# Joint statistics for the first four token tiles, and transposes of the identity on TensorE at the start of a transformer block

## The chip, the cores and the metric

The kernel runs on one core of a Trainium2 chip. The metric is the device time of one launch in microseconds (us). A core has five engines that run their own instruction queues: TensorE (PE; its weight loads are shown as PEld), VectorE (DVE), ScalarE (ACT), GpSimd (POOL) and SyncE (SP), which here issues the DMA transfers. Engines wait for each other by semaphores.

## The reference

The reference is one transformer block on 2048 tokens of width 512, in float32. Cut to what matters here:

```python
xn = _layernorm(x, axis=-1)
x = x + _L0_attn_ref(xn, w_qkv, w_o) + _L0_ffn_ref(xn, gate, up, down)   # 4-bit FFN weights

def _layernorm(x, axis=-1, eps=1e-05):
    m = jnp.mean(x, axis=axis, keepdims=True)
    v = jnp.var(x, axis=axis, keepdims=True)
    return (x - m) / jnp.sqrt(v + eps)
```

Attention is causal with 16 heads of width 32; the feed-forward part has width 4096. Both take the same normalized tokens.

## The kernel before, in words

The tokens stand in 16 tiles of 128 tokens by 512 values, and four tiles make a token block (`b` = 0 to 3). All instructions are recorded in a fixed order by hand, so each engine runs its own in the order in which the Python code calls them.

At the start, constants are made: GpSimd writes `ident`, the 128 by 128 identity (line 130). SyncE issues the loads: token tiles `x0` to `x3`, the projection weights `wqk` of the first group of heads, the value weights `wv` in four parts, then `x4` to `x15` (lines 62 to 71). The tiles use eight buffers in turn, so the load of `x8` waits until `x0` has been normalized, and so on.

A token block then goes through three helpers:

- `statistics(b, first, n)` computes mean and variance of `n` tiles on VectorE (`st`, line 468, and `mv`, line 469, for each tile), and then the inverse standard deviation for all `n` at once: `ve` (line 471), a square root on ScalarE (`sd`, line 473), and five small operations on VectorE (`q` and `rstd`, lines 476 to 481) that refine and invert it.
- `normalize(b, i)` writes the normalized tile `xn` on VectorE (line 489), in one of two buffers (`turn12`, `turn13`).
- `flip(b, i)` transposes `xn` on TensorE in four pieces of 128 by 128, with `ident` as the other operand, to the PSUM tile `ptx` (line 505), and ScalarE copies that to `xnT` (line 508).

For the first block this is done for two tiles at a time:

```python
for i in range(4):
    if i % 2 == 0:
        statistics(0, i, 2)
    normalize(0, i)
    flip(0, i)
```

Then follows a loop over the four blocks. For each it records the next block's `statistics` and first `normalize`, two projections of the present block (`project`, line 166, queries and keys of the first heads, each with a copy on ScalarE at line 178 or 180), and then four steps of transposes of the next block, scores (line 210), their row maxima on VectorE and values (`ps_v`, line 516). A projection is four float32 matmuls of 128x128 by 128x512, which the profile shows as eight instructions.

After this stage come the attention of the pairs of heads, the output projection and the feed-forward part, in which no line is touched by the change. PSUM tiles named `t` come from a pool of three buffers, `ps_t`, which the attention uses in turn.

Of the kernel before, what the change touches and what calls it, by code (L numbers as in the profile page):

```python
# [46 lines left out]
P = 128  # L47
# [7 lines left out]
NK = H // P  # L55
# [23 lines left out]
def block_kernel(  # L79
# [10 lines left out]
    nc = tc.nc  # L90
# [4 lines left out]
    def turn_tile(i, name, dtype=F32, shape=(P, TB)):  # L95
        return turns.tile(list(shape), dtype, tag=f"turn{i}", name=name)
# [17 lines left out]
    with (  # L114
# [14 lines left out]
        ident = const.tile([P, P], F32, tag="ident", name="ident")  # L129
# [69 lines left out]
        def tile_of(pool, name):  # L199
            return pool.tile([P, TB], F32, tag="s" if pool is ps_s else "t", name=name)  # L200
# [262 lines left out]
        def statistics(b, first=0, n=4):  # L463
            key = f"{b}_{first}"
            mv = small.tile([P, n, 2], F32, tag="mv", name=f"mv{key}")
            for i in range(n):
                st = small.tile([P, 6], F32, tag="st", name=f"st{key}_{i}")
                nc.vector.bn_stats(st, xs[4 * b + first + i])
                nc.vector.bn_aggr(mv[:, i, :], st)
            ve = small.tile([P, n], F32, tag="ve", name=f"ve{key}")  # L470
            nc.vector.tensor_scalar(ve, mv[:, :, 1], EPS, None, ALU.add)
            sd = small.tile([P, n], F32, tag="sd", name=f"sd{key}")
            nc.scalar.activation(sd, ve, AF.Sqrt)

            q = small.tile([P, n], F32, tag="q", name=f"q{key}")
            nc.vector.reciprocal(q, sd)
            nc.vector.tensor_tensor(q, q, ve, ALU.mult)
            nc.vector.tensor_tensor(q, q, sd, ALU.add)
            nc.vector.tensor_scalar(q, q, 0.5, None, ALU.mult)
            rstd = small.tile([P, n], F32, tag="rstd", name=f"rstd{key}")  # L480
            nc.vector.reciprocal(rstd, q)
            for i in range(n):
                mvs[b, first + i], rstds[b, first + i] = mv[:, i, 0:1], rstd[:, i : i + 1]
# [1 line left out]
        xns = {}  # L485

        def normalize(b, i):
            xn = turn_tile(12 + i % 2, f"xn{b}_{i}", shape=(P, NK, 8, 16))
            nc.vector.tensor_scalar(
                xn,  # L490
                xs[4 * b + i].rearrange("p (b r k) -> p k r b", b=16, r=8),
                mvs[b, i],
                rstds[b, i],
                ALU.subtract,
                ALU.mult,
            )
            xns[b, i] = xn

        def flip(b, i):

            bank = i % 2 if b == 0 else b < 3
            pt = ps_m.tile([P, TB], F32, tag=f"m{int(bank)}", name=f"ptx{b}_{i}")
            xn = xns.pop((b, i))
            for k in range(NK):
                nc.tensor.transpose(  # L505
                    pt[:, k * P : (k + 1) * P], xn[:, k].rearrange("p r b -> p (r b)"), ident
                )
            nc.scalar.copy(
                xnT[b][:, :, i * P : (i + 1) * P],
                pt.rearrange("p (k t) -> p k t", k=NK),  # L510
            )

        def value_halves(t):
# [11 lines left out]
            nc.scalar.copy(v[t // 4][:, t % 4, :], ps)  # L525
            yield

        for i in range(4):
            if i % 2 == 0:
                statistics(0, i, 2)  # L530
            normalize(0, i)
            flip(0, i)

        later = [(1, b, which) for b in range(NTB) for which in range(2)]
        for b in range(NTB):
            n = first[b]
            if b + 1 < NTB:
                statistics(b + 1)
                normalize(b + 1, 0)
            project(0, b, 0)  # L540
            project(0, b, 1)
            for i in range(4):
                if b + 1 < NTB:
                    flip(b + 1, i)
                full_width = [value_halves(4 * b + i)] * 2
                if b >= 2:
                    full_width += [project_halves(*later.pop(0))] * 2
                for j in range(b + 1):
                    rows_when_due()
                    tiles = [score_rows(0, n, ps_s), score_rows(1, n, ps_t)]  # L550
                    for p in range(2):
                        maxima(p, n, tiles[p])
                    if j == 0 and i < 3 and b + 1 < NTB:
                        normalize(b + 1, i + 1)
                    n += 1
                    for _ in range(-(-len(full_width) // (b + 1 - j))):
                        next(full_width.pop(0))
# [13 lines left out]
        for m in range((NP - 2) * STEPS):  # L571
            p, n = divmod(m, STEPS)
# [36 lines left out]
            if own in places and og + 2 < NOG:  # L609
                b, which = places[own]  # L610
                project(og + 2, b, which, tile_of(ps_s, f"ps_qk{og + 2}_{b}_{which}"))
            if own in places_own and og > 0 and og + 1 < NOG:
                b, which = places_own[own]
# [56 lines left out]
        for s, n in enumerate(together):  # L670
# [21 lines left out]
            if early and s % 2 == 0 and not diagonal(together[s + 1]):  # L692
                i, k = early.pop(0)
                b = ORDER[i]
# [178 lines left out]
    with tc.manual_schedule():  # L873
# [13 lines left out]
        for n, t in enumerate(order):  # L887
# [13 lines left out]
            if n < 8:  # L901
                b, k = ORDER[2 + n // NK], n % NK
# [180 lines left out]
```

## Time and profile before

| what | value |
|---|---|
| median of 3 runs | 1975.38 us (1973.5 to 1975.81) |
| profiled execution | 1972.27 us, of which the span is 1970.2 us |
| TensorE busy in the span | 1934.5 us (98%) |
| VectorE, ScalarE, GpSimd busy | 67%, 56%, 47% |
| data moved by DMA | 39.86 MB |
| mean granted TensorE clock | 0.999 |

Busy time is the time in which an engine has an instruction at work; matmuls overlap each other, and a busy TensorE is not TensorE at its peak. Times in the timeline and the chain of waits are microseconds from the start of the span: first the start, then the time taken, then engine, tile and line. A line of the timeline may sum up several instructions (`x8`), and in square brackets is the engine's idle time before it and what ended it. In a table of windows, PEclk is the granted clock of TensorE as a share of full speed, the third value from the end of a line.

### The profile page before, as it was taken

The numbers are of one execution on the slowest core, as the hardware profiler recorded it, in microseconds if no ns is written. First come the engines' busy times: TensorE is split into PE (matmuls) and PEld (weight loads), VectorE is DVE, ScalarE is ACT, GpSimd is POOL, SyncE is SP. The second block draws the span as 40 slices with busy tenths as digits, with TensorE's granted clock in tenths as the row PEclk, the third lists the DMA queues.
The fourth block names the chain that finished last, engine by engine and source line by source line (L and its number), as shares of the span: only waits on it lengthen the run. The fifth ranks groups of instructions, "written<-read, shape, count | busy, mean of one in ns | idle before, by whom it ended". The sixth has DMA issues, their size and how long they took to land.

```text
span 1970.2 us, 32411 instructions
## 1 busy us (share of the span) xinstructions
PE 1934.5 (98%) x11648; PEld 1182.9 (60%) x11648; DVE 1326.7 (67%) x2706; ACT 1104.2 (56%) x2299; POOL 927.6 (47%) x1055
## 2 busy tenths in 40 slices
PE   7999999999999999999999999999999999999998
PEld 3433333333333332247888888888888888888886
DVE  5657665656555764187777676777777777777774
ACT  2112665656556666625666666666666666666664
POOL 1001555545445653155655454555555555555451
PEclk9999999999999999999999999999999999999999
DMA  3000000000000000020000000000000000000002
GB/s 128 0 11 11 2 2 1 1 12 2 1 1 12 2 1 21 18 79 22 22 18 23 19 22 20 21 20 20 19 22 20 21 21 21 21 19 24 18 5 86
DMA packets 55392, 39.86 MB, mean 20 GB/s; under 512 B 14784, under 2 KB 47552, under 8 KB 55232
## 3 DMA queue, kind: packets, MB, share of 16 engines
q1 hardware_dynamic: 55232, 37.81, 6.5%
q8 instruction: 91, 1.49, 0.3%
q14 instruction: 69, 0.57, 0.1%
HBM read 33.55 MB, written 4.19 MB: 19 GB/s over the span
## 4 chain that ended last, share of the span: by engine, by line
PE 94%; ACT 3%; POOL 1%; issue 1%; DVE 1%; DMA 0%; DVEq 0%; ACTq 0%; POOLq 0%
PE gu L935 24%; PE gu L948 12%; PE pd L998 12%; PE av L344 10%; PE ps_s L210 8%; PE pd L1010 6%; PE ps_qk L166 6%; PE ps_t L281 4%; PE ps_t L296 3%; PE ps_v L516 3%; PE po L890 3%; ACT prob L310 2%; POOL added L396 1%; PE ptx L505 0%; PE pm L262 0%
## 5 line engine op out<-in xcount | busy, mean ns | idle before, releaser
L935 PE MATMUL gu<-xh,gu 128*128 128x512 f32 x1024 | 403.9, 394 | 0.0
L935 PE MATMUL gu<-lm,gu 128*128 128x512 f32 x1024 | 403.7, 394 | 0.0
L234 DVE TENSOR_REDUCE tops<-ps_s 128x1 f32<-128x512 f32 x384 | 243.7, 682 | 160.4 <-PE ps_s L210 122.3
L1019 DVE SCALAR_TENSOR_TENSOR acc<-pd,acc 128x512 f32<-128x512 f32 x512 | 317.1, 682 | 2.4 <-PE pd L1010 2.4
L980 POOL TENSOR_TENSOR parts<-inter,hi 128x512 fp32r<-128x512 f32 x128 | 171.1, 1336 | 278.2 <-DVE hi L976 271.9
L310 ACT ACTIVATE prob<-ps_t 128x512 f32<-128x512 f32 x384 | 205.7, 596 | 145.6 <-PE ps_t L296 102.1
L210 PE MATMUL ps_s<-qk,qk 32*128 32x512 f32 (+3 forms) x1280 | 286.4, 576 | 0.0
L948 PE MATMUL gu<-lm,gu 128*128 128x512 f32 x1024 | 279.7, 395 | 0.0
L972 DVE SCALAR_TENSOR_TENSOR inter<-gu,gate 128x512 f32<-128x512 f32 x128 | 88.5, 692 | 274.9 <-PE gu L948 274.9
L296 PE MATMUL ps_t<-qk,qk 32*128 32x512 f32 (+3 forms) x1280 | 271.2, 538 | 0.0
L1005 ACT ACTIVATE pd<-pd 128x512 f32<-128x512 f32 x512 | 263.4, 583 | 1.1 <-PE pd L998 1.1
L344 PE MATMUL av<-prob,v 128*32 128x128 f32 (+3 forms) x1856 | 257.6, 425 | 5.5 <-ACT both L430 4.2
L998 PE MATMUL pd<-wd,parts 128*128 128x512 f32 x1024 | 259.6, 396 | 0.0
L942 ACT ACTIVATE gu<-gu 128x512 f32<-128x512 f32 x256 | 148.7, 581 | 188.2 <-PE gu L935 188.1
L396 POOL TENSOR_TENSOR added<-prob,prob 128x512 f32<-128x512 f32 x144 | 179.6, 1268 | 115.9 <-ACT prob L310 115.4
L948 PEld LDWEIGHTS gu<-lm,gu 128*128 128x128 f32 x1024 | 192.0, 188 | 47.1 <-issue 0.2
L935 PEld LDWEIGHTS gu<-lm,gu 128*128 128x128 f32 x1024 | 191.9, 187 | 46.6 <-POOL wd L805 0.2
L998 PEld LDWEIGHTS pd<-wd,parts 128*128 128x128 f32 x1024 | 192.3, 188 | 45.8
L935 PEld LDWEIGHTS gu<-xh,gu 128*128 128x128 f32 x1024 | 192.0, 188 | 45.7 <-ACT wd L804 0.2
L344 PEld LDWEIGHTS av<-prob,v 128*32 128x32 f32 x1856 | 67.2, 108 | 206.2 <-issue 147.5
L229 DVE CUSTOM_DVE_ANT_0 ps_s<-ps_s,mask_qk 128x128 f32<-128x128 f32 (+3 forms) x256 | 120.8, 516 | 92.0 <-PE ps_t L296 52.3
L979 ACT CAST parts<-hi 128x512 fp32r<-128x512 f32 x128 | 79.7, 623 | 173.2 <-DVE hi L976 171.4
(106 smaller groups left out, 2942.8 us busy)
## 6 DMA issues: line engine op xcount, KB each, us to landing
pk<-packed SPq DMA_DIRECT2D x96, 128.0 KB, 2.2
sc<-scales SPq DMA_DIRECT2D x512, 8.0 KB, 1.6
x<-x SPq DMA_DIRECT2D x16, 256.0 KB, 3.5
acc<-x SPq DMA_DIRECT2D x16, 256.0 KB, 3.3
sc<-scales SPq DMA_DIRECT2D x256, 16.0 KB, 1.7
out<-acc SPq DMA_DIRECT2D x16, 256.0 KB, 2.2
wqk<-w_qk SPq DMA_DIRECT2D x4, 512.0 KB, 3.7
wv<-w_v SPq DMA_DIRECT2D x4, 256.0 KB, 5.4
```

What stands on the lines that cost most here:

```text
L210: nc.tensor.matmul(ps[:, :w], lhsT=qT[p // 2, qb][rows, i * P : (i + 1) * P], rhs=kT[p // 2, c][rows, :w], start=True, stop=True,)
L234: nc.vector.tensor_reduce(top, ps[:, :w], AX.X, ALU.max)
L296: nc.tensor.matmul(ps[:, c0:], lhsT=kT[p // 2, kt // 4][rows, (kt % 4) * P : (kt % 4 + 1) * P], rhs=qT[p // 2, qb][rows, c0:], start=False ...
L310: nc.scalar.activation(prob[:, h, :], ps, AF.Exp)
L344: nc.tensor.matmul(avs[p, qb][D * j : D * (j + 1), c0:c1], lhsT=v[kt // 4][:, kt % 4, D * head : D * (head + 1)], rhs=prob[:, h, c0:c1], s ...
L396: nc.gpsimd.tensor_tensor(t, prob_a[:, h], prob_b[:, h], ALU.add)
L935: nc.tensor.matmul(ps, lhsT=parts[:, i, k], rhs=mov, start=(k == 0 and i == 0), stop=(k == NK - 1 and i == 1),)
L948: nc.tensor.matmul(ps, lhsT=gu[g, m, j][:, 2, k], rhs=lm[b, k][1], start=False, stop=(k == NK - 1), skip_group_check=True,)
L980: nc.gpsimd.tensor_tensor(parts[:, 1], inter, high, ALU.subtract)
L998: nc.tensor.matmul(po, lhsT=parts[:, part, i * P : (i + 1) * P], rhs=w[:, part], start=(part == 0), stop=(part == 1),)
L1005: nc.scalar.activation(po, po, AF.Copy, scale=HIGH_SCALE)
L1019: nc.vector.scalar_tensor_tensor(acc[t], po, SUM_SCALE, acc[t], ALU.mult, ALU.add)
```

## The change

The statistics of the first block's four tiles are taken in one call, ahead of the four normalizations. The first block's normalized tiles get four buffers instead of two. And TensorE is given 36 transposes of the identity, written to a PSUM tile `idle` that nobody reads, ahead of the first tokens, three more after each of the first three tiles' transposes, and six after the last. `idle` is a tile of the pool `ps_t`, and so takes one turn of its three buffers.

```diff
         def normalize(b, i):
-            xn = turn_tile(12 + i % 2, f"xn{b}_{i}", shape=(P, NK, 8, 16))
+            xn = turn_tile(12 + i % (2 if b else 4), f"xn{b}_{i}", shape=(P, NK, 8, 16))
...
+        idle = tile_of(ps_t, "idle")
+
+        def stay_busy(n):
+
+            for _ in range(n):
+                nc.tensor.transpose(idle[:, :P], ident, ident)
+
+        stay_busy(36)
+        statistics(0)
         for i in range(4):
-            if i % 2 == 0:
-                statistics(0, i, 2)
             normalize(0, i)
             flip(0, i)
+            stay_busy(3 if i < 3 else 6)
```

In the instruction order of the two kernels, TensorE has 51 transposes more (36, 3, 3, 3 and 6), VectorE has six instructions fewer and ScalarE one fewer. The first transpose of the identity waits for GpSimd alone. The two normalizations that waited for TensorE to release a buffer of `xn` no longer do. All other instructions stand in the same order with the same waits.

## The prediction

> **What bounds the kernel.** I read the page's chain and slices first, then the chain of the first 50 us in order of time, then the timeline of the start.
>
> ```profile
> PE   7999999999999999999999999999999999999998
> ...
> PE 94%; ACT 3%; POOL 1%; issue 1%; DVE 1%; DMA 0%; DVEq 0%; ACTq 0%; POOLq 0%
> ```
>
> TensorE is on the chain for 94% of the span, and only the first slice (49 us) has room. The edit touches nothing behind the first projection, so it is worth what it moves that projection, and how fast that runs. The chain of 0 to 50 us:
>
> ```profile
> 0.80 2.64 DMA x<-x
> 3.47 0.71 DVE st L468
> ...
> 6.64 0.75 DVE xn L489
> 7.39 0.14 issue
> 7.53 1.95 PE ptx L505 x8
> 9.50 0.58 ACT xnT L508
> 10.09 0.11 ACT sd L473
> ...
> 11.30 0.75 DVE xn L489
> 12.05 0.14 issue
> 12.18 1.96 PE ptx L505 x8
> 14.16 0.59 ACT xnT L508
> 14.76 0.04 issue
> 14.80 5.22 PE ps_qk L166 x8
> 20.04 0.61 ACT qk L178
> 20.65 0.04 issue
> 20.69 3.71 PE ps_qk L166 x8
> ```
>
> Until 14.80 us the chain is VectorE's: statistics of two tiles, two normalized tiles, then both again, with the transposes and a ScalarE copy behind each pair. From 14.80 it is TensorE with its copies, and no load is in it after the first token tile. So a shift at 14.80 reaches the end whole: I find nothing behind that would absorb it.
>
> The same eight matmuls take 5.22 us, and 3.71 us right after. The timeline of weight loads shows the step:
>
> ```profile
> 16.67 0.34 PEld L166 LDWEIGHTS ps_qk<-xnT,wqk 128*128 128x128 f32 x1 [0.52 <-issue]
> 17.52 0.34 PEld L166 LDWEIGHTS ps_qk<-xnT,wqk 128*128 128x128 f32 x1 [0.52 <-issue]
> 18.13 0.19 PEld L166 LDWEIGHTS ps_qk<-xnT,wqk 128*128 128x128 f32 x1 [0.27 <-issue]
> 18.56 0.19 PEld L166 LDWEIGHTS ps_qk<-xnT,wqk 128*128 128x128 f32 x1 [0.24 <-issue]
> ```
>
> Starts stand 0.85 us apart, then 0.61, then 0.43: TensorE doubles its pace at about 17.9 us, some 3.07 us after its first dense matmul. The transposes show the same two paces: starts 0.213 us apart in the two early groups, 0.109 us in the groups from 25.07 on. The column of granted clock says 1.00 even for 14.80 to 16.50, so it doesn't show this step at the start; it does show the way back, at the end:
>
> ```profile
> 1963.40:1966.88 3.48, 1.73 (x7) 0.70 (x5) 2.75 (x5) 1.17 (x3) 0.00 (x0) 1.00 0.74 273
> 1966.88:1970.20 3.32, 0.00 (x0) 0.00 (x0) 0.00 (x0) 0.00 (x0) 0.00 (x0) 0.50 0.54 201
> ```
>
> The last matmul starts at 1964.62, and at 1966.88 the granted clock is 0.50.
>
> **VectorE's part.** One set of six small operations and one square root go (in the second pair, 9.69 to 11.30 us), and statistics of x2 and x3 come ahead of the first normalization. Statistics start 0.82, 0.80 and 0.79 us apart, so x3's would start at 5.88; its landing is recorded at 6.07 us (x2's at 4.83, in time), so it starts at 6.10. That added wait holds what is queued behind it on VectorE, all on the path, and costs 0.2 us. From a last statistics to ve is 0.91 us (15.03 to 15.94), from ve to xn 1.44 (first pair) to 1.54 us (four wide, with one more wait in it): xn0 starts at 8.45 to 8.55, I take 8.48, and the next 0.65 us apart, xn3 at 10.4 instead of 11.95. From xn's start to its first transpose is 0.88 us (6.64 to 7.53), so the first real transpose can go at 9.36 us.
>
> Hidden: statistics of the next block start at 11.1, when x4 has landed (10.97) and x5 to x7 come at 11.66 to 13.01 us, before each is read; their xn is wanted by TensorE only after both projections. The loads of x8 and later wait on SyncE for xn0 and on (x8 now until 9.2 us instead of 7.4), and behind them stand the other loads; DMA is full with earlier tiles until about 13 us, and x8 is first read at 42.5 us. Were that cover gone, 2 us would show. ScalarE loses one 0.2 us operation; GpSimd's work is unchanged. Two more xn buffers take away two waits.
>
> **TensorE's part.** The 36 transposes need only the identity, written by 1.37 us; the first starts at about 1.46. Nothing real is queued behind them before 9.36. At the slow pace they last 36 x 0.213 = 7.67 us, until 9.15, 0.2 us before the tokens. That is 2.5 times the 3.07 us after which the matmuls sped up. Whether transposes bring the faster pace can't be read here: two groups stood dense for 1.7 us each without it, which is shorter than 3.07. I bound it both ways.
>
> If they count, the step comes after 3 to 6 us, the 36 end between 6.6 and 8.3 us, and a tile costs TensorE (4 + 3) x 0.109 + 0.03 = 0.79 us, a little over VectorE's 0.65. So the tiles go at 9.36, 10.15, 10.94 and 11.73; the last transpose of ptx3 starts at 12.07, the copy 0.31 later (25.46 to 25.76) at 12.37, the projection 0.64 after that (14.16 to 14.80), at 13.01. The six last idle ones end at 12.8 and are under the copy. The projection starts 1.79 us earlier, and runs 3.74 us to its copy (20.69 to 24.43) instead of 5.24 (14.80 to 20.04): 1.50 us. Sum **-3.29 us**.
>
> If they don't, the pace stays slow, a tile costs 7 x 0.213 + 0.03 = 1.52 us, TensorE and no longer VectorE sets the order, ptx3 starts at 9.36 + 3 x 1.52 = 13.92, and the six last ones hold the projection until 13.92 + 0.88 + 6 x 0.213 = 16.08: **+1.28 us** at least.
>
> [...]
>
> I take the first value: in both states matmuls and transposes change pace together and by the same factor (0.85 to 0.43, 0.213 to 0.109), and 36 stand dense for longer than the matmuls needed.
>
> **Time.** The profiled execution took 1972.27 us, 2.07 outside its span; less 3.29 it is 1968.98. The three runs' median is 1975.38, 3.1 us above that execution, from which I carry the difference over: 1972.1 us. With a pace change that came later, all eight matmuls of the first projection would start 0.853 us apart and take some 7.2 us instead of 5.24; executions like that would gain 1.79 + 3.46 = 5.25 us. [...] About 0.2% (3.95 us) is what a measurement of this kernel can tell from no change.
>
> **Rivals.**
> 1. *Transposes don't count* (chance 0.25). For it: no speed-up in either early group. Price +1.28 us; if the slow stretch also takes in the whole first projection, 1.96 more, +3.2. The slower side: it decides when starts stay above about 0.175 us apart, since 9.36 + 31 x 0.175 = 14.8. 1976.7 to 1978.6 us.
> 2. *The pace is lost again in the gap between the 36 and the tokens* (0.12). The gap is 1.1 to 2.7 us, and at the end of the trace the clock was halved within 2.3 us of the last matmul's start. Then the tokens' transposes start slow and speed up after 3 to 6 us: a speed-up at 12.4 gives a start at 14.5 and a fast projection, -1.8; one that comes only just before the projection -0.2. I take -1.0: 1974.4. Against it: with the step at 4.2 us and later the TensorE stands still for under 3 us.
> 3. *The edit moves nothing* (0.03): the extra transposes start late, or x3 lands later. 1975.4.
>
> **Numbers.** Forecast 1972.1 with 0.60. Its gain is 2.8 to 5.25 us by execution, and it passes 3.95 in somewhat under half: 0.27 of the 0.60. Faster: 0.27 + 0.02 (rival 2) + 0.01 = 0.30. Slower by over 0.2%: 0.05 of rival 1, with the three runs' own scatter (2.3 us), + 0.02. The rest, 0.63, within 0.2%. The forecast's own range is 1969.6 (gain 5.25, less 0.5 of scatter) to 1973; up to 1977.4 takes in rival 2 and over half of rival 1, leaving out some 2 in 10.
>
> **What would show it.** Right: statistics x4 in a row, xn at about 8.5; the 36 end between 6.6 and 8.3; ptx groups of 0.6 us, not 0.85; first projection from 13.0, weight loads 0.43 apart from the first on, and 3.7 us. Wrong: the 36 at 0.213 to the end at 9.15, ptx groups 1.5 us apart, projection after 16; or a fast stretch and slow tokens (rival 2). A time beyond 1979 or below 1969 would mean that something behind 50 us moved, which I can't see.

## The result, and the profile after

| | median | runs |
|---|---|---|
| before | 1975.58 us | 1972.21 to 1976.27, 12 runs |
| changed | 1971.66 us | 1968.85 to 1972.91, 12 runs |

The ratio is 0.9981, with a 95% interval of 0.9973 to 0.9988: some 3.9 us faster (2.4 to 5.3). 3.29 us were forecast, 1972.1 us. The profiled execution of the changed kernel took 1971.69 us, with a span of 1969.6, only 0.6 us shorter than before's; the reason is a fall of the clock at the start of the attention, shown below.

From the profile's page of the changed kernel, the slices of TensorE and the chain's shares:

```profile
PE   8999999999999999999999999999999999999998
...
PE 94%; ACT 3%; POOL 1%; issue 1%; DVE 0%; DMA 0%; SPq 0%; DVEq 0%; ACTq 0%; POOLq 0%
```

The first slice goes from 7 to 8 tenths busy, the transposes of the identity included; the rest is as before. The chain of waits of the first 30 us (start, time, what):

```profile
2.18 4.13 DMA x<-x
6.30 0.02 issue
6.33 0.70 DVE st L468
...
8.74 0.75 DVE xn L489
9.49 0.04 issue
9.53 0.66 PE ptx L505 x4
10.19 0.33 PE idle L533 x3
10.51 0.44 PE ptx L505 x4
...
12.04 0.44 PE ptx L505 x4
12.48 0.66 PE idle L533 x6
13.13 0.02 issue
13.15 3.71 PE ps_qk L166 x8
16.87 0.02 issue
16.89 0.61 ACT qk L178
17.50 0.04 issue
17.54 3.71 PE ps_qk L166 x8
```

The chain now begins with the load of the fourth tile (6.30), goes through one set of statistics, and then through TensorE. The first projection starts at 13.15 instead of 14.80 and takes 3.71 instead of 5.22 us. The next block's first transposes start at 21.92 instead of 25.07: **3.15 us earlier**, and from here on both kernels do the same.

A table of windows of the changed kernel (busy time and count for each engine; the granted clock is third from the end) shows the step of the pace under the 36 transposes, and what comes later:

```profile
1.40:5.30 3.90, 3.88 (x18) 3.88 (x19) 2.15 (x8) 0.68 (x1) 2.28 (x6) 1.00 0.78 252
5.40:7.40 2.00, 2.00 (x19) 1.85 (x17) 1.63 (x5) 0.00 (x0) 0.00 (x0) 1.00 0.99 359
...
189.80:196.40 6.60, 6.28 (x35) 1.82 (x29) 2.76 (x5) 2.30 (x6) 3.63 (x4) 0.50 0.00 0
196.60:200.00 3.40, 3.23 (x40) 1.23 (x34) 1.41 (x4) 2.51 (x7) 1.21 (x2) 1.00 0.00 0
```

Eighteen transposes touch the first 3.9 us, nineteen the next 2.0. In the trace their starts stand 0.213 us apart until 5.3 and 0.109 us from 5.5 on, and the trace's record of the granted clock begins at 5.39 us. That record starts with the first change of the clock, and the table shows 1.00 for all time ahead of it, whatever the pace; in before's trace it starts at 17.87 us, where the matmuls doubled their pace. Up to 5.39 us TensorE had done nothing but transpose the identity. The third line is new: from 189.7 to 196.5 us the granted clock is 0.50, at the start of the attention loop. Before's profile has 1.00 there:

```profile
189.80:196.40 6.60, 4.63 (x37) 1.73 (x36) 4.03 (x8) 4.16 (x9) 2.49 (x2) 1.00 0.15 61
```

### The profile page after: what moved, and what is told of

It reads as the page before. It is cut to its first block, busy times and chain, and to the rows that moved or that the text cites. A ratio compares the mean times of both kernels' runs of the same rounds, so it can differ in the third digit from the quotient of the medians.

```text
span 1969.6 us, 32503 instructions
## 1 busy us (share of the span) xinstructions
PE 1941.5 (99%) x11699; PEld 1188.9 (60%) x11699; DVE 1325.7 (67%) x2700; ACT 1104.7 (56%) x2298; POOL 927.8 (47%) x1055
## 4 chain that ended last, share of the span: by engine, by line
PE 94%; ACT 3%; POOL 1%; issue 1%; DVE 0%; DMA 0%; SPq 0%; DVEq 0%; ACTq 0%; POOLq 0%
PE gu L943 24%; PE gu L956 12%; PE pd L1006 12%; PE av L344 10%; PE ps_s L210 8%; PE pd L1018 6%; PE ps_qk L166 6%; PE ps_t L281 4%; PE ps_t L296 3%; PE ps_v L516 3%; PE po L898 3%; ACT prob L310 2%; POOL added L396 1%; PE ptx L505 0%; PE pm L262 0%
```

## Experiments

**Joint statistics alone** (e1): the joint statistics and the four buffers stay, the transposes of the identity go, and with them the tile `idle` and its turn in the pool.

```diff
-        idle = tile_of(ps_t, "idle")
...
-        stay_busy(36)
         statistics(0)
         for i in range(4):
             normalize(0, i)
             flip(0, i)
-            stay_busy(3 if i < 3 else 6)
```

> The joint statistics and the four buffers of xn alone, no transposes of the identity. Theory (the transposes bring TensorE to its fast pace, the joint statistics only bring xn earlier): xn0 starts at 8.7 us as in the changed kernel, but the transposes of the tokens stand 0.213 us apart, so a tile costs 0.85 us and the last one starts at 9.53 + 0.24 + 14 x 0.213 = 12.75; copy at 13.2, first projection at 13.85 (before 14.80, after 13.15), and its matmuls start slowly, 0.85 us apart for 3 to 6 us, so that it takes 5.2 to 7.2 us to its copy instead of 3.74. The next block's first transposes then come at 24.1 to 26.1 us (before 25.07, after 21.92): some 1 us gained, or as much lost. Rival (joint statistics alone bring the gain, the pace would have come anyway): next block's transposes at about 22 us.

Its timeline of TensorE:

```profile
10.00 3.73 PE L505 MATMUL ptx<-ident,xn 128*128 128x128 f32 x16 [10.00 <-DVE xn L489]
14.41 1.98 PE L166 MATMUL ps_qk<-xnT,wqk 128*128 128x512 f32 x4 [0.68 <-ACT xnT L508]
```

The tokens' sixteen transposes are slow, 0.213 us apart, as expected, and the projection starts at 14.41 (0.47 of its delay is a later first tile, 10.00 instead of 9.53). But it is fast from the first matmul: the pace changed at 14.33 us in the record. Sixteen slow transposes in one piece, 3.3 us, had brought it, just in time. Next block's transposes: 23.17, 1.90 us earlier than before. I had expected at most 1. So joining the statistics does two things: it brings the last tile earlier, and it puts the transposes in one dense piece. Its single run took 1970.26 us.

**The transposes of the identity alone** (e2): statistics in pairs and two buffers, as before.

> The 51 transposes of the identity alone; statistics in two pairs and two buffers of xn as before. Theory with the pace held: xn2 and xn3 as before at 11.3 and 11.95, last transposes of ptx3 at 13.3, copy 13.6, projection at 14.25 and fast (3.74): next block's first transposes at 23.0 us, 2.1 earlier than before and 1.1 later than after. Theory with the pace lost: between the pairs TensorE stands still from about 9 to 12.2 us, and if that is long enough the second pair is slow again (0.213 us apart), the projection starts at 15.4 to 15.8 and its matmuls are slow: next block's first transposes at 25.7 or later. Which of the two it is tells how long a gap the pace outlasts.

```profile
8.81 0.60 PE L505 MATMUL ptx<-ident,xn 128*128 128x128 f32 x4
9.25 0.49 PE L533 MATMUL idle<-ident 128*128 128x128 f32 x3
12.25 0.63 PE L505 MATMUL ptx<-ident,xn 128*128 128x128 f32 x4 [2.51 <-DVE xn L489]
...
13.47 0.82 PE L533 MATMUL idle<-ident 128*128 128x128 f32 x6
14.31 1.98 PE L166 MATMUL ps_qk<-xnT,wqk 128*128 128x512 f32 x4
```

The pace came at 6.86 us and outlasted the gap between the pairs (2.51 us). The projection starts at 14.31 (expected 14.25), next block's transposes at 23.08 (expected 23.0): 1.99 us earlier than before. The two parts alone give 1.90 and 1.99, together 3.15, since both remove the same 1.50 us of slow matmuls. Counted once, that leaves 2.39; the other 0.76 lies in the start of e1's projection, which was late by 0.47 us for its first tile and by 0.79 for its slow transposes, and 0.49 of that is in e2's gain already. Its single run, 1972.85 us, has the fall of the clock at the start of the attention in it (191.2 to 198.0 us), as the changed kernel's profile has, and e1's hasn't; so the times of single runs can't be set against each other, and the place of the next block's transposes can.

**Eight or twenty in front instead of 36** (e3, e5):

```diff
-        stay_busy(36)
+        stay_busy(8)       # e5: stay_busy(20)
```

> The changed kernel with 8 instead of 36 transposes of the identity in front; all else as in it. They end at 1.43 + 0.24 + 7 x 0.213 = 3.2 us, and TensorE then stands still for 6.3 us. Theory (it is the length of dense work that brings the pace): the tokens' transposes and those of the identity between them are slow, a tile costs 7 x 0.213 = 1.5 us, ptx3 starts at about 14.0 unless the pace comes within that stretch, projection between 14.5 and 16.3: this is the slower side of the prediction, next block's first transposes at 23.3 (pace comes before the projection) to 26.6 us. Rival (any early use of TensorE is enough, or the pace depends on the time since the start): as the changed kernel, 21.9 us.

> The changed kernel with 20 instead of 36 transposes of the identity in front. They end at 5.6 us if all are slow, earlier only if the pace comes within them; then TensorE stands still for some 4 us, where it was 2.0 us in the changed kernel and 2.75 us between the two pairs with the identity's transposes alone, and neither lost the pace. Theory (a gap of a whole stretch of 3.4 us or more takes the pace back, or too few transposes don't bring it): the tokens' transposes start 0.213 us apart, and the projection starts at 14.5 or later, next block's first transposes at 23 us or later. Rival (the pace outlasts 4 us): as the changed kernel, 21.9 to 22.3 us.

With eight, the transposes of the first three tiles are slow and TensorE sets the order: groups start at 9.74, 11.29 and 12.78, 1.5 us apart, as the slower rival of the prediction had it. The pace comes at 13.46, just before the projection at 15.16; next block's at 23.93. With twenty it comes at 6.67, after the last one has started (5.53), and is gone again when the tokens come. Windows of the run with twenty:

```profile
6.70:10.05 3.35, 0.06 (x1) 0.07 (x2) 2.75 (x10) 0.20 (x1) 0.00 (x0) 1.00 1.03 388
10.10:13.45 3.35, 3.35 (x17) 3.35 (x18) 3.28 (x7) 1.17 (x2) 0.00 (x0) 0.50 1.05 391
13.55:20.00 6.45, 5.74 (x25) 3.20 (x24) 3.32 (x12) 1.98 (x4) 0.00 (x0) 1.00 0.41 139
```

An empty stretch of 3.41 us at the full clock, then one at half clock under dense slow transposes, then full again; next block's transposes at 24.04. So an early use of TensorE wasn't enough in these two runs: the eight brought no faster pace ahead of the tokens, and what the twenty brought was gone after the gap. Gaps of 2.0 us in the changed kernel and 2.5 us in e2 did no harm, 4.0 us lost the pace in this execution. The single runs took 1973.57 us (e3, with the clock's fall at the attention, 191.0 to 197.8) and 1971.23 us (e5, without it).

**More transposes at the start of the attention** (e4, on the changed kernel; e7, on before). There TensorE waits for exponentials between narrow matmuls (1.19, 0.54 and 0.53 us in before's profile).

```diff
+        idle_av = ps_m.tile([P, TB], F32, tag="m0", name="idle_av")
+        fill = {0: 10, 1: 5, 2: 5}
         for m in range((NP - 2) * STEPS):
...
             rows_when_due()
...
             later_on(3, attend_diagonal, p, n, prob)
...
+            for _ in range(fill.get(m, 0)):
+                nc.tensor.transpose(idle_av[:, :P], ident, ident)
```

> The changed kernel with 10, 5 and 5 transposes of the identity more behind the first three steps of the attention loop, where TensorE waits 1.19, 0.54 and 0.5 us for exponentials. In the profiled execution of the changed kernel the granted clock is 0.50 from 189.7 to 196.5 us, in that of before it isn't; the transposes of the second block stand 3.15 us earlier in the changed kernel, at 196 us only 0.7 us earlier. The changed kernel's runs have two levels, 1969 and 1972 us. Theory (the lower clock there is the difference of the levels, and it comes when a stretch of some 3.4 us has too little TensorE work): the granted clock stays at 1.00 from 185 to 197 us in this kernel, its runs are all at 1969 to 1969.7 us, median 2.5 us under the changed kernel's 1971.66 and 6 us under before. Rival (the levels have another cause, and the drop costs nothing in the end): runs still at 1969 and 1972, or all 1 to 2 us above these for the added work.

> The kernel before with nothing changed but the 10, 5 and 5 transposes of the identity behind the first three steps of the attention loop. Theory (before loses the granted clock there too, in most of its executions, and its two levels of 1975.5 and 1972.2 us are with and without that): the granted clock stays at 1.00 from 185 to 200 us, median 1972.3 us, some 3 us under before, though the start is as before; what is left of spread comes from the slow stretch at the start. Rival (the fill helps the changed kernel only, because its attention starts earlier): median as before, 1975.

From the first matmul of the attention to the next transposes of `parts` (line 262), the same work takes 8.38 us in before (188.05 to 196.43), 10.81 in the changed kernel's profile with the lower clock (184.89 to 195.70), and 8.39 with the fill on either kernel (185.14 to 193.53 and 188.35 to 196.74). So the lower clock there costs 2.4 us and the fill nothing. That too little work in some 3.4 us brings the lower clock was the expectation's theory; what these profiles show is that it didn't come with the fill. e4 ran at 1968.97 to 1969.50 us but for one run at 1971.03, median 1969.37, ratio to before 0.9976 (0.9966 to 0.9986): the level above 1971.6, which 7 of the changed kernel's 12 runs had, is in none of these nine. The mean granted clock on record says the same of every run: 0.998 in those seven, 0.999 or 1.000 in the five others and in all of e4's (6.83 us at half clock take 0.0017 off the mean).

On before the expectation was missed: median 1973.71 beside 1973.91 for before on the same chip, ratio 0.9996 (0.9987 to 1.0005). What the fill took away is the top: 12 of before's 27 runs there are over 1975 us, all with a mean clock of 0.998; none of e7's 11 is over 1974.3, and none has a mean clock below 0.999. So before, too, has executions in which the clock falls, though its profile is none of them. What was wrong is where the others lie: ten of the eleven are at 1973.1 to 1974.3, and one is at 1972.4. The profile shows one reason, another place where the clock falls:

```profile
752.00:755.60 3.60, 2.64 (x32) 0.96 (x28) 2.29 (x7) 3.12 (x7) 0.87 (x3) 1.00 0.00 0
755.70:759.00 3.30, 3.30 (x16) 0.64 (x16) 2.58 (x4) 1.94 (x4) 2.15 (x3) 0.50 0.00 0
```

Against before's profile, which has 1.00 there, it is 0.31 us late ahead of this stretch (749.21 for 748.90) and 1.99 behind it (759.19 for 757.20): 1.7 us lost. Whether that makes up the rest of its spread isn't shown.

**Joint statistics with the fill** (e8): e1 with the same fill, which leaves the start alone to differ.

> The joint statistics and four buffers with the fill in the attention loop, without the transposes of the identity at the start. In its one execution without the fill, 16 slow transposes of the tokens stood dense for 3.3 us and brought the pace just ahead of the projection, which then ran fast: next block's first transposes at 23.2 us. Theory (that hangs on when in those 3.4 us the tokens come, and varies by execution): times from 1969.5 (pace before the projection) to 1971.5 us (after 3 us of slow matmuls), median 1 to 2 us over the changed kernel with the fill (1969.4). Rival (the tokens' own transposes always bring the pace, the identity's are needless): median 1970.3 at most and little spread.

Median 1970.58 us, from 1969.95 to 1974.05; six runs lie at 1969.9 to 1970.6, three at 1972.2 to 1972.3, two over 1973. Here the tokens' own transposes must bring the pace. In the profiled execution they did at 13.06, ahead of the projection; that they come too late in the runs above 1972 is likely, but no profile of such a run shows it. Beside before with the fill on the same chip (1973.71) joint statistics give about 3.1 us by medians. Against the changed kernel with the fill (1969.37, on another chip) the identity's transposes give 1.2 us more; 0.73 of it stands in the two profiles (next block's transposes at 22.94 and 22.21), and the runs above 1972 are gone. On a third chip the changed kernel with the fill had a median of 1970.32 (e11 below), so this 1.2 is no firm number.

**Two versions meant to be faster** (e6, e10), and the changed kernel and e4 again beside the second (e9, e11). e10 has the fill, 44 transposes in front, none between the tiles; e6 also moves two loads to ScalarE's queue.

```diff
-        stay_busy(36)
+        stay_busy(44)
...
-            stay_busy(3 if i < 3 else 6)
+        stay_busy(6)                      # behind the loop
...
-            nc.sync.dma_start(out=xt, ...)
+            queue = nc.scalar if t in (1, 3) else nc.sync      # e6 alone
+            queue.dma_start(out=xt, ...)
```

> A version meant to be faster than both: the changed kernel with the fill, 44 instead of 36 transposes of the identity in front, none between the tiles and six at the end, and the loads of x1 and x3 issued by ScalarE's queue, so that four loads are issued by 1.7 instead of 2.6 us. x3 was waited for until 6.1 to 6.7 us in the runs with joint statistics. Theory: x3 lands by 5.5 us, xn0 starts at 8.1 instead of 8.7, the tiles follow VectorE's 0.65 us instead of 0.76, so ptx3's last transposes start 1 us earlier; next block's first transposes at 20.9 us, median 1968.4 us (1969.4 with the fill alone). Rival (the loads share the same bandwidth and x3 lands no earlier; the thinner stretch between tiles loses the pace): 1969.2 to 1971.

> The changed kernel itself, on one chip with the two versions below, for a comparison side by side. Theory (two levels by whether the granted clock falls at the start of the attention): runs at 1969 and 1971.5 to 1973 us, median about 1971.7.

> The changed kernel with the fill, 44 transposes of the identity in front, none between the tiles, six at the end; the loads as in the changed kernel. Theory: the tiles follow VectorE's 0.65 us instead of TensorE's 0.76, so the projection starts 0.3 to 0.4 us earlier than with the fill alone, median 1969.0 us; where the last xn comes at 10.9, projection at 12.8. Rival (the thinner stretch loses the pace in some executions): a second level some 1.5 us higher.

> The changed kernel with the fill of e4 again, beside the two above on one chip. Theory: 1969.0 to 1969.5 us but for a run or two, 2 to 2.5 us under the changed kernel's median here. Rival (the fill's gain was the chip's): the same median as the changed kernel here.

e6: median 1969.64 us (1968.4 expected), ratio 0.9977 (0.9968 to 0.9986), no better than e4; next block's transposes at 22.43 (20.9 expected). The loads did harm. VectorE's timeline:

```profile
4.61 0.69 DVE L469 BATCH_NORM_STATS2 st<-x 128x6 f32<-128x512 f32 x1 [2.81 <-DMA x<-x]
```

Its first tile comes at 4.6 instead of 3.5 us, the first xn starts at 9.41 instead of 8.74. Issued together, the first two tiles landed at 4.59 and 4.81 us instead of 3.46 and 4.09. The fourth landed a little earlier (6.02 instead of 6.30), but VectorE, which began 1.1 us later, only came to it at 7.03. That fits loads that share a bandwidth; no run tests it.

e9, e10 and e11 on one chip: medians 1971.85, 1969.05 and 1970.32 us, ratios to before 0.9979 (0.9971 to 0.9988), 0.9969 (0.9957 to 0.9982) and 0.9977 (0.9966 to 0.9987). e10 is the fastest by median, where it was expected (1969.0); the intervals overlap. Its profile holds a surprise:

```profile
4.30:11.00 6.70, 4.61 (x40) 4.09 (x38) 5.48 (x16) 0.67 (x2) 0.00 (x0) 1.00 0.99 339
11.10:14.40 3.30, 3.19 (x16) 3.11 (x16) 3.12 (x9) 1.78 (x4) 0.00 (x0) 0.50 1.05 397
```

In this execution the pace was lost at 11.05, under the tokens' transposes; the projection started at 14.33 and was fast again from 14.46. That is the prediction's second rival, in a variant of the change. The gap ahead of the tokens, 2.05 us, was as long as in the changed kernel (2.04 us), which kept the clock with three transposes of the identity between the tiles. But e6 had none between the tiles either and kept it (next block's transposes at 22.43). So the missing transposes alone don't explain it, and what else played a part isn't shown. e10's other five runs lie at 1969.03 to 1969.13 us, so that the three transposes between the tiles pay isn't shown. e11 lies higher than e4 (1969.32 to 1971.78 against 1968.97 to 1971.03), so the fill's gain is 1.5 us here, side by side, and 2.3 between the first runs of the changed kernel (1971.66) and e4. e11's five upper runs have a mean granted clock of 0.999, its three lowest 1.000, which fits 3.41 us at half clock, as in e10's profile (11.05 to 14.46), by an estimate from the span (0.0009 of the mean); where it would be isn't shown.

e9's profile shows the other level of the changed kernel. Its windows:

```profile
185.00:190.00 5.00, 3.27 (x26) 1.27 (x29) 2.21 (x5) 3.77 (x6) 1.76 (x9) 1.00 0.35 110
190.00:197.00 7.00, 6.30 (x66) 2.50 (x67) 4.37 (x9) 4.50 (x11) 4.85 (x4) 1.00 0.00 0
```

The same kernel without the fall of the clock: 8.39 us for that stretch, and a span of 1967.4 us. That is 2.2 less than in the first profile, though its start was 0.4 us later (next block's transposes at 22.33).

## Why the prediction was right, step by step

- *VectorE's chain.* xn0 at 8.74 for 8.48: x3 landed at 6.30 where before had 6.07, and the last statistics started at 6.33 for 6.10. In the other runs with joint statistics and the loads as they were, xn0 was 0.2 to 0.7 us later. The added wait for a load was rightly found, as a fixed 0.2 us for x3; it is 0.27 to 0.99 us by execution, and in the other runs it is mostly x2 that is waited for (it landed at 5.56 to 6.15 us, where before had 4.83).
- *The idle transposes count.* The step that decides, taken at 0.60 against 0.25. It holds: in the seven profiles with 36 or 44 in front the pace came at 4.2 to 7.4 us, 2.8 to 6.0 us after their start (3 to 6 forecast; the 3 is the 3.07 us of before's matmuls, the 6 was the author's estimate, which no run of before shows). Of 36 the last one started between 7.2 and 8.2 us, where the slow pace throughout would give 8.9. The forecast for their end, 6.6 to 8.3 us, should by its own terms begin at 6.9 (14 slow, 22 fast); the gap of up to 2.7 us in the second rival is then at most 2.5.
- *A tile at 0.79 us.* Groups start at 9.53, 10.35, 11.11 and 11.88: 0.82 and then 0.76. The projection at 13.15 for 13.01, and 3.74 us to its copy (13.15 to 16.89), to the hundredth. The six last transposes were hidden under the copy: from the copy's start to the projection is 0.63 us (12.52 to 13.15), 0.64 in before. The chain above names them because by their modelled ends they stop 0.02 us ahead of the projection; its weight load waited for the copy.
- *The sum.* -3.29 forecast, -3.15 at 21.92 us: 1.65 for the earlier start (1.79 forecast) and 1.50 for the matmuls (1.50). That executions of before with all eight matmuls slow would gain 5.25 us stays open: the two profiles with before's start, before and e7, both have the step inside the projection.
- *"Nothing behind that would absorb it"* was wrong. In the profiled execution the attention's start gave back 2.4 of the 3.15 us, which the profile of before couldn't show, as it had no such fall. Both kernels have executions of several levels, so the medians still differ by 3.9 us; the 0.6 above the forecast lies within the interval, and I can't put it to a cause.
- *The time* is right in part by luck. 1972.1 us were reached by carrying over the 3.1 us between before's median and its profiled execution, with no cause for them. The runs show levels behind them: 10 of before's 12 runs are over 1975 us, 7 of the changed kernel's 12 over 1971.6. That most runs of both kernels would be in the upper level was not foreseen; had they differed in this, the medians would have moved by something else than what the start gained.
- *Rival 1* showed its order and its spacing of 1.5 us only where the transposes in front were too few (e3, e5). *Rival 2* didn't happen in the profiled executions of the change, but in e5 and e10.

## What to carry to other kernels

On a kernel that TensorE bounds, look at the spacing of the first matmuls, not only at busy time: here the doubled spacing cost 1.50 us of the first projection, and idle TensorE time ahead of it bought that back with work that nobody needs, these transposes, where it was dense for long enough and reached close enough to the real work: 36 of them (some 6 us) with a gap of 2 us did; 8 (2 us) didn't bring the pace in time, and behind 20 a gap of 4 us lost it. Then look for other thin stretches of TensorE (narrow matmuls with waits): here the clock fell there in some executions, and twenty transposes in the waits cost nothing (8.39 us for that stretch with them, 8.38 in before's profile without). When runs of one kernel come in levels, one profile may show either; compare a part of the trace, not one span with another.

## What the runs showed of the hardware

- *When the full clock came.* With 36 or 44 transposes in front, which started at 1.42 or 1.43 us in these profiles, the record of the granted clock has it at 4.22, 5.39, 6.26, 6.45, 6.78, 6.86 and 7.38 us. Stretches of constant clock between two recorded changes lasted, for instance, 1949.01 us in before, 184.32, 6.83 and 1771.52 us in the changed kernel and 3.41 us in e10. What sets the moment of a change isn't shown.
- *TensorE was not busy right up to the rise in every run.* In e1 the clock rose at 14.33 us although the slow transposes had ended at 13.73 by the modelled ends; from 10.90 to 14.30 us TensorE was busy for 2.83 us. In e5 it rose at 6.67 us, and the last of the twenty had ended at 5.95. In before the two groups of eight slow transposes, with 1.94 us of busy time each (from 7.53 and from 12.18 us), were followed by no rise; it came at 17.87 us, 3.07 us after the first matmul.
- *Nor was TensorE empty ahead of every fall.* In e5 it was (0.06 us busy from 6.70 to 10.05). At the start of the attention the clock fell at 189.7 us in the changed kernel's profile, behind waits of 1.19 and 0.54 us, in the middle of a busy kernel: from 186.30 to 189.70 us TensorE was busy for 1.67 us, and the clock was low for 6.83 us. In e9, the same kernel, it stayed at 1.00 there. In e7 the clock fell at 755.7 us after 2.64 us of busy time from 752.00 to 755.60; before's profile, 0.31 us ahead in this work, has 2.59 us there and no fall. What decides between the two levels of a kernel isn't shown.
